# Attention over edges in layer 0: where the edge's direction is multiplied in, and which groups of rows and columns TensorE uses

## The chip, the cores and the metric

The kernel runs on one core of one Trainium2 chip. The metric is device time in microseconds (us), the median of several executions. The profile is one more execution, recorded by the hardware profiler.

## The reference, cut to what matters

A graph network of four layers runs over 6,250 nodes (64 scalars and 32 vectors of three components each, 160 numbers) and 100,000 edges sorted by their end node. Each layer gathers node features at the edges' ends, forms a product with the edge's direction, sums over the edges of each node, and is followed by a layer norm. Only layer 0, attention with four heads, is changed. For each edge with `y0` (a number) and `y1` (three numbers), and weights `w1 = rbf @ W_rbf` (224 columns from 16 inputs):

```
msg      = (source features) + (end features)                      # s: 64, v: 32 x 3
m1_s     = [w_ss*s*y0,  w_vv0*(v . y1)/sqrt3]                      # 96 scalars
m1_v     = [(w_sv*s) y1,  w_vs*v*y0,  w_vv1*(v x y1)/sqrt2]        # 128 vectors
a        = sum over 16 of leaky(m1_s @ W_alpha) * alpha_dot         # 4 heads
alpha    = softmax of a over the edges of one end node
val_s    = m1_s @ Ws_val;   val_v = (m1_v @ Wv_val) * sigmoid(val_s @ Wg);   val_s = sigmoid(val_s)
m2_s, m2_v = the same product of val with y0, y1, and learned constants
h        = [m2_s @ Ws_vlin,  m2_v @ Wv_vlin]                        # per head 16 + 8 x 3
out      = sum over edges of alpha * h, then Wps and Wpv, added to the node
```

## The kernel before, in words

Edges are padded to 784 chunks of 128. The edge loop of layer 0 (`edge_loop0`) takes windows of three chunks (WC = 3, 384 edges), 262 of them, and a window writes to at most 32 consecutive end nodes (WM = 32). It is a software pipeline: step s loads window s, and other parts of the work are done for windows s-2 to s-10 in the same step. Inside `tc.manual_schedule()` the order in which the calls stand in the loop body is the order of each engine's queue; each engine works its queue strictly in that order and waits on semaphores for the others.

The parts of a window, with their lines in the profile:

- `radial` (L1399 to L1417), once in four steps: SP loads the 16 edge inputs and the transposed `y` rows, and POOL multiplies them (L1416), so that a row of 128 partitions holds the inputs times each of the four directions.
- `load` (L1203): POOL gathers three chunks of source features and 32 end-node rows (L722); SP loads the end nodes' numbers, from which `masks` (L1217, DVE) builds `on`, 1 where an edge belongs to a node; `others` (L1222, ACT) makes a large negative number elsewhere.
- `ends` (L1229, PE): end features by a matmul of `on` with the 32 rows. `weights` (L1239, PE): the radial weights for all four directions, in four row groups of 32. `features` (L1249, DVE) adds the ends to the source features.
- `product1` (L1258 to L1263, L1186, L1191): the first product on DVE and POOL, into `tp`, 480 columns.
- `turn` (L1288, L1290): four transposes of a chunk, and ACT's copy `xt`. `linear` (L1296, L1298): the matmuls into `z`, ACT's tanh `th` (L1299) and copy `la` (L1300). `gated` (L1303, DVE). `score` and `spread` (L1314 to L1323).
- `scores`, `exps` (L1330 to L1343): scores by node and edge, their maximum, the exponentials `pT`. `by_edge` (L1352, L1354): `pT` transposed to edges.
- `product2` (L1272 to L1276): the second product, on DVE and POOL, into `m2`, 481 columns (the last is one, for the denominators).
- `sums` (L1359, L1362): `p` times `m2`, over the window's edges. `channels` (L1367 to L1371) turns the sums, `outputs` (L1377 to L1392) multiplies by the last weights, `write` (L735, SP) stores the row.

[...]

The lines that set the gathered rows and PSUM buffers are few:

```
self.wy = self.ps.tile([P, 4, 512], F32, name="wy", bufs=1)
pt = self.ps.tile([P, 4, P], F32, name="t", bufs=2)
z = self.z = self.ps.tile([P, 256], F32, name="z", bufs=1)
self.pa = self.ps.tile([P, 481], F32, name="m", bufs=1)
```

Of the kernel before, what the change touches and what calls it, by code (L numbers as in the profile page):

```python
# [11 lines left out]
I32 = mybir.dt.int32  # L12
# [32 lines left out]
def kernel(ctx: ExitStack, tc: tile.TileContext, t: dict, out: bass.AP):  # L45
# [80 lines left out]
    y_rows = dram.tile([NCH * 4, P], F32, name="y_rows")  # L126
# [11 lines left out]
    with tc.tile_pool(name="prep", bufs=1) as prep:  # L138
# [35 lines left out]
        y4 = prep.tile([P, NCH, 4], F32, name="y4")  # L174
        vec.tensor_copy(y4, y5[:, :, 0:4])
        with tc.tile_pool(name="prep_ps", bufs=2, space=PSUM) as ps, tc.tile_pool(name="prep_sb", bufs=3) as sb:
            for c in range(0, NCH, 32):
                m = min(32, NCH - c)
                pt = ps.tile([P, P], F32, name="pt")
                pe.transpose(pt[0 : 4 * m, :], y4[:, c : c + m, :].rearrange("p c i -> p (c i)"), ident)  # L180
                yt = sb.tile([P, P], F32, name="yt")
                act.copy(yt[0 : 4 * m, :], pt[0 : 4 * m, :])
                nc.sync.dma_start(y_rows[4 * c : 4 * (c + m), :], yt[0 : 4 * m, :])
# [7 lines left out]
    win0G = const.tile([WM, NW0], I32, name="win0G")  # L191
# [3 lines left out]
    with tc.tile_pool(name="win", bufs=1) as sb, tc.tile_pool(name="winp", bufs=1, space=PSUM) as ps:  # L195
# [73 lines left out]
        vec.tensor_copy(win0G, nb[0:WM, :])  # L269
# [912 lines left out]


    def dotted(o, x, n):
        b = x.rearrange("p c i (j k) -> p c (i j) k", k=V)
        vec.tensor_reduce(o[:, 0:n, 3, S:96], b[:, 0:n, 0:9:4, :].rearrange("p c b k -> p c k b"), AX.X, ALU.add)  # L1186

    def crossed(o, x, n, eng):
        b = x.rearrange("p c i (j k) -> p c (i j) k", k=V)
        for k, (p, q) in enumerate(((7, 5), (2, 6), (3, 1))):  # L1190
            eng.tensor_tensor(o[:, 0:n, k, 96:P], b[:, 0:n, p, :], b[:, 0:n, q, :], ALU.subtract)  # L1191

    class Window0:
# [3 lines left out]
        def __init__(self, w, sb, ps, n, yr, at, gi, y, rows, ids, node_idx, dst, tps):  # L1197
            self.w, self.sb, self.ps, self.n = w, sb, ps, n
            self.yr, self.at = yr, at
            self.gi, self.y, self.ids, self.node_idx, self.dst = gi, y, ids, node_idx, dst  # L1200
            self.rows, self.tps = rows, tps

        def load(self):  # L1203
# [3 lines left out]
            self.fw = sb.tile([WM, F], F32, name="fw", bufs=5)  # L1207
# [17 lines left out]
        def ends(self):  # L1225

            self.fd = self.ps.tile([P, WC * F], F32, name="m", bufs=1)
            for c in range(self.n):
                pe.matmul(self.fd[:, c * F : (c + 1) * F], self.on[0:WM, c * P : (c + 1) * P], self.fw, start=True, stop=True)  # L1229

        def weights(self):

            n, w = self.n, self.w
            self.wy = self.ps.tile([P, 4, 512], F32, name="wy", bufs=1)
            half, c0 = self.at
            for c in range(n):
                for i in range(4):
                    q = slice(i * 32, (i + 1) * 32)
                    pe.matmul(  # L1239
                        self.wy[:, i, c * F : (c + 1) * F],  # L1240
                        self.yr[q, (c0 + c) * P : (c0 + c + 1) * P],
                        w["rbf"][q, half, :],
                        start=True,
                        stop=True,
                    )

        def features(self):
            n = self.n
            vec.tensor_add(self.f[:, 0:n, :], self.f[:, 0:n, :], self.fd[:, 0 : n * F].rearrange("p (c q) -> p c q", q=F))  # L1249
            self.tp = next(self.tps[0])  # L1250

        def product1(self):

            n, f = self.n, self.f[:, 0 : self.n]
            o = self.tp.rearrange("p c (b q) -> p c b q", b=4)
            wy = self.wy[:, :, 0 : WC * F].rearrange("p b (c q) -> p c b q", q=F)[:, 0:n]
            x = self.sb.tile([P, WC, 3, 3 * V], F32, name="x1", bufs=2)
            yield vec.tensor_mul(o[:, 0:n, :, 0:S], bc(f[:, :, 0:S], 2, 4), wy[:, :, :, 0:S])  # L1258
            yield vec.tensor_mul(x[:, 0:n], bc(f[:, :, S:F], 2, 3), wy[:, :, 0:3, S:F])
            yield crossed(o, x, n, pool)  # L1260
            fv = f[:, :, S:F].rearrange("p c (j k) -> p c j k", k=V)
            wv = wy[:, :, 3, S:F].rearrange("p c (j k) -> p c j k", k=V)
            yield vec.tensor_mul(o[:, 0:n, 0:3, S:96], fv, wv)  # L1263
            yield dotted(o, x, n)

        def product2(self):

            n, v, y = self.n, self.val[:, 0 : self.n], self.y
            m2 = self.m2 = next(self.tps[1])
            o = m2.rearrange("p c (b q) -> p c b q", b=4)  # L1270
            x = self.sb.tile([P, WC, 3, 3 * V], F32, name="x2", bufs=2)
            yield vec.tensor_mul(o[:, 0:n, :, 0:S], bc(v[:, :, 0:S], 2, 4), bc(y, 3, S))  # L1272
            yield vec.tensor_mul(x[:, 0:n], bc(v[:, :, S:F], 2, 3), bc(y[:, :, 0:3], 3, 3 * V))
            yield crossed(o, x, n, pool)
            vv = v[:, :, S:F].rearrange("p c (j k) -> p c j k", k=V)
            yield vec.tensor_mul(o[:, 0:n, 0:3, S:96], vv, bc(y[:, :, 3:4].to_broadcast([P, n, 3]), 3, V))  # L1276
            yield dotted(o, x, n)

        def turn(self, c):

            if c == 0:
                self.la = self.sb.tile([P, WC, S], F32, name="la", bufs=2)
                self.val = self.sb.tile([P, WC, F], F32, name="val", bufs=3)
                self.th = self.sb.tile([P, WC, 96], F32, name="th", bufs=2)
                self.xt = {}
            pt = self.ps.tile([P, 4, P], F32, name="t", bufs=2)
            for k in range(4):
                pe.transpose(pt[:, k, :], self.tp[:, c, k * P : (k + 1) * P], ident)  # L1288
            self.xt[c] = self.sb.tile([P, 4, P], F32, name="xt", bufs=3)
            act.copy(self.xt[c], pt)  # L1290

        def linear(self, c):

            w, xt = self.w, self.xt.pop(c)
            z = self.z = self.ps.tile([P, 256], F32, name="z", bufs=1)
            pe.matmul(z[:, 0:F], xt[0:96, 3, :], w["ms"], start=True, stop=True)  # L1296
            for k in range(3):
                pe.matmul(z[:, F + k * V : F + (k + 1) * V], xt[:, k, :], w["mv"], start=True, stop=True)  # L1298
            act.activation(self.th[:, c, :], z[:, S:F], AF.Tanh, scale=0.5)  # L1299
            act.copy(self.la[:, c, :], z[:, 0:S])  # L1300

        def gated(self, c):
            vec.scalar_tensor_tensor(  # L1303
                self.val[:, c, S:F].rearrange("p (k v) -> p k v", k=3),
                bc(self.th[:, c, S:96], 1, 3),
                1.0,
                self.z[:, F:256].rearrange("p (k v) -> p k v", k=3),
                ALU.add,
                ALU.mult,
            )  # L1310

        def score(self):
            n, w, sb = self.n, self.w, self.sb
            act.activation(self.val[:, 0:n, 0:S], self.th[:, 0:n, 0:S], AF.Copy, bias=1.0)  # L1314
            vec.scalar_tensor_tensor(self.la[:, 0:n], self.la[:, 0:n], 0.2, self.la[:, 0:n], ALU.mult, ALU.max)
            vec.tensor_mul(self.la[:, 0:n], self.la[:, 0:n], bc(w["adot"], 1, n))
            self.sc = sb.tile([P, WC, 4], F32, name="sc", bufs=2)
            vec.tensor_reduce(self.sc[:, 0:n], self.la[:, 0:n].rearrange("p c (h a) -> p c h a", h=4), AX.X, ALU.add)  # L1318

        def spread(self):  # L1320
            n = self.n
            self.sca = self.sb.tile([P, WC, P], F32, name="sc_all", bufs=2)
            pool.tensor_copy(self.sca[:, 0:n].rearrange("p c (h m) -> p c h m", h=4), bc(self.sc[:, 0:n], 3, WM))  # L1323

        def scores(self):

            n = self.n
            pt = self.ps.tile([P, 4 * P], F32, name="t", bufs=2)
            for c in range(n):
                pe.transpose(pt[:, c * P : (c + 1) * P], self.sca[:, c, :], ident)  # L1330
            self.spt = pt

        def exps(self, old=None):
            n, sb, e, pt = self.n, self.sb, self.n * P, self.spt
            s = sb.tile([P, WC * P], F32, name="s", bufs=2)
            mx = self.row[:, 41:42]
# [10 lines left out]

        def by_edge(self):
            n, e = self.n, self.n * P
# [3 lines left out]
            self.p = self.sb.tile([P, WC * P], F32, name="p", bufs=2)  # L1353
            act.copy(self.p[:, 0:e], pt[:, 0:e])  # L1354

        def sums(self, c):
            if c == 0:
                self.pa = self.ps.tile([P, 481], F32, name="m", bufs=1)
            pe.matmul(self.pa, self.p[:, c * P : (c + 1) * P], self.m2[:, c, 0:481], start=c == 0, stop=c == self.n - 1)  # L1359
            if c == self.n - 1:  # L1360
# [547 lines left out]
```

## Time and profile before

| | |
|---|---|
| time, median of 3 runs | 8017.31 us (8013.19 to 8020.87) |
| the profiled execution | 8008.86 us, its span 8007.1 us |
| mean granted clock of TensorE | 0.948 |
| layer 0's edge loop, first to last transpose (L1288) | 315.0 to 3261.0 us |
| steps between these | 261 |
| DMA, mean over the span | 100 GB/s |

The page names engines: PE is TensorE's matmuls, PEld its weight loads, DVE VectorE, ACT ScalarE, POOL GpSimd, SP SyncE. A line of a group gives line, engine, operation, out<-in, shapes and count, then busy us and the mean ns of one, then the engine's idle time just before and what ended most of it. In a listing by time the first number is the start, the second the length of one or several instructions that follow each other. Matmuls overlap, so the distance from start to start says more of them than the length.

### The profile page before, as it was taken

The numbers are of one execution on the slowest core, as the hardware profiler recorded it, in microseconds if no ns is written. First come the engines' busy times: TensorE is split into PE (matmuls) and PEld (weight loads), VectorE is DVE, ScalarE is ACT, GpSimd is POOL, SyncE is SP. The second block draws the span as 40 slices with busy tenths as digits, with TensorE's granted clock in tenths as the row PEclk, the third lists the DMA queues.
The fourth block names the chain that finished last, engine by engine and source line by source line (L and its number), as shares of the span: only waits on it lengthen the run. The fifth ranks groups of instructions, "written<-read, shape, count | busy, mean of one in ns | idle before, by whom it ended". The sixth has DMA issues, their size and how long they took to land. (4 is left out here: it accounts for less than half of the span.)

```text
span 8007.1 us, 150406 instructions
## 1 busy us (share of the span) xinstructions
PE 7328.2 (92%) x49240; PEld 5720.5 (71%) x49240; DVE 5391.7 (67%) x11871; ACT 3997.6 (50%) x12138; POOL 5269.2 (66%) x5412
## 2 busy tenths in 40 slices
PE   4899999999999999789999999997888887888887
PEld 2677877787878878569999999995555556555556
DVE  5488888878888788557777777775444446555557
ACT  1255555555555555345555555555555554333334
POOL 0377777777777777117777777772777770677771
PEclk9999999999999999669999999996899998999999
DMA  4344444433333333235565656555333335444446
GB/s 137 99 121 111 112 116 119 109 61 63 60 64 60 64 60 63 53 103 99 100 103 98 100 101 100 98 88 144 87 86 86 86 85 178 112 110 110 110 110 228
DMA packets 645090, 799.53 MB, mean 100 GB/s; under 512 B 185122, under 2 KB 512146, under 8 KB 636722
## 3 DMA queue, kind: packets, MB, share of 16 engines
q1 hardware_dynamic: 404818, 501.89, 22.3%
q0 software_dynamic: 238880, 283.36, 20.5%
q8 instruction: 402, 6.59, 0.4%
q14 instruction: 414, 3.39, 0.1%
q10 hardware_dynamic: 576, 4.30, 0.1%
HBM read 548.48 MB, written 240.64 MB: 99 GB/s over the span
## 5 line engine op out<-in xcount | busy, mean ns | idle before, releaser
L722 POOL DMA_INDIRECT f<-feat,r_src x2352 | 2536.4, 1078 | 969.7 <-issue 550.8
L1081 POOL DMA_INDIRECT tab<-o,scat x784 | 1350.4, 1722 | 433.5 <-ACT o L1080 301.5
L857 PE MATMUL pa<-pr,oy 128*128 128x321 f32 (+1 forms) x3136 | 1110.6, 492 | 0.0
L866 ACT COPY o<-pa 32x96 f32<-32x96 f32 (+4 forms) x2358 | 553.3, 245 | 843.4 <-PE pa L857 797.1
L1067 PE MATMUL pt<-same,tp 128*128 128x128 f32 x6272 | 895.5, 286 | 7.0 <-DVE tp L710 4.0
L857 PEld LDWEIGHTS pa<-pr,oy 128*128 128x128 f32 x3136 | 609.4, 199 | 371.0 <-issue 193.7
L1067 PEld LDWEIGHTS pt<-same,tp 128*128 128x128 f32 x6272 | 764.3, 192 | 24.2 <-PE pf L1051 16.3
L1290 ACT COPY xt<-t 128x512 f32<-128x512 f32 x784 | 460.8, 588 | 592.6 <-PE t L1288 568.7
L1359 PE MATMUL m<-m,p 128*128 128x481 f32 x1568 | 739.0, 581 | 0.9 <-ACT row L1390 0.9
L1069 ACT COPY xt<-pt 128x512 f32<-128x512 f32 x784 | 459.6, 586 | 524.3 <-PE pt L1067 524.3
L1298 PEld LDWEIGHTS z<-w_mv,xt 128*128 128x128 f32 x4704 | 622.1, 195 | 0.0
L1078 PE MATMUL po<-ov,xt 128*128 128x32 f32 x4704 | 611.6, 267 | 0.0
L1323 POOL COPY sc_all<-sc 128x384 f32<-128x384 f32 x262 | 302.8, 1156 | 464.2 <-DVE sc L1318 461.3
L1298 PE MATMUL z<-w_mv,xt 128*128 128x32 f32 x4704 | 601.5, 265 | 0.0
L1078 PEld LDWEIGHTS po<-ov,xt 128*128 128x128 f32 x4704 | 588.3, 192 | 0.0
L807 PE MATMUL ww<-w,hid 64*128 64x192 f32 (+1 forms) x2088 | 260.8, 364 | 297.1 <-DVE pr L839 170.7
L1288 PE MATMUL t<-ident,tp 128*128 128x128 f32 x3136 | 513.9, 288 | 0.0
L1288 PEld LDWEIGHTS t<-ident,tp 128*128 128x128 f32 x3136 | 385.3, 152 | 178.1 <-issue 126.1
L807 PEld LDWEIGHTS ww<-w,hid 64*128 64x128 f32 x2088 | 180.8, 189 | 443.9 <-ACT o L866 208.5
L1303 DVE SCALAR_TENSOR_TENSOR val<-th,z 128x96 f32<-128x96 f32 x784 | 196.3, 250 | 406.6 <-ACT la L1300 406.2
L846 DVE TENSOR_TENSOR pr<-f,ww 128x384 f32<-128x384 f32 x131 | 72.7, 555 | 561.8 <-DMA f<-feat,r_src 255.2
L1299 ACT ACTIVATE th<-z 128x96 f32<-128x96 f32 x784 | 197.0, 251 | 433.9 <-PE z L1298 396.3
(328 smaller groups left out, 16509.6 us busy)
## 6 DMA issues: line engine op xcount, KB each, us to landing
tab<-zeros SPq DMA_DIRECT2D x49, 1280.0 KB
nodes<-in_src_row_dram SPq DMA_DIRECT2D x98, 512.0 KB
dn<-in_dst_row_dram SPq DMA_DIRECT2D x261, 192.0 KB
f<-feat,r_src POOLq DMA_INDIRECT x2352
tb<-tab SPq DMA_DIRECT2D x24, 1280.0 KB
e<-in_ef64T_dram SPq DMA_DIRECT2D x196, 128.0 KB
dn<-in_dst_row_dram SPq DMA_DIRECT2D x196, 128.0 KB
e<-in_ef64T_dram SPq DMA_DIRECT2D x261, 96.0 KB
```

Of the source, the lines that this page charges most:

```text
L722: pool.indirect_dma_start(out=o, out_offset=None, in_=table, in_offset=bass.IndirectOffsetOnAxis(ap=idx, axis=0),)
L807: pe.matmul(self.ww[:, q, 0:wn], self.hid[k, c * P : (c + 1) * P], m, start=True, stop=True)
L857: pe.matmul(pa[:, 0:m], self.oy[:, q, :], self.pr[:, q, 0:m], start=c == 0, stop=c == self.ns[h] - 1)
L866: act.copy(o[q, at : at + e], pa[q, b0 * V : b0 * V + e])
L1067: pe.matmul(pt[:, k, :], self.tp[:, c, lo : lo + P], self.same[:, c, :], start=True, stop=True)
L1069: act.copy(self.xt, pt)
L1078: pe.matmul(po[:, 96 + i * V : 96 + (i + 1) * V], xt[:, 1 + i, :], w["ov"], start=True, stop=True)
L1081: pool.indirect_dma_start(out=self.tables[c % len(self.tables)], out_offset=bass.IndirectOffsetOnAxis(ap=self.scat[:, c : c + 1], axis=0), ...
L1288: pe.transpose(pt[:, k, :], self.tp[:, c, k * P : (k + 1) * P], ident)
L1290: act.copy(self.xt[c], pt)
L1298: pe.matmul(z[:, F + k * V : F + (k + 1) * V], xt[:, k, :], w["mv"], start=True, stop=True)
L1359: pe.matmul(self.pa, self.p[:, c * P : (c + 1) * P], self.m2[:, c, 0:481], start=c == 0, stop=c == self.n - 1)
```

## The change

All of it lies in layer 0.

- The weights are no longer multiplied by the directions beforehand. `radial` multiplies the inputs by `y0` alone, and lays the three chunks of a window in three row groups of 32 (16 rows times `y0`, 16 without). The gather of end rows brings them three times (96 rows), and `ends` makes end features and weights in three row groups, into three banks `wf`.
- The first product multiplies features by weights only (384 columns in `tp` instead of 480), but for the dot product, which DVE and POOL make with `y1`. `linear` multiplies three transposed pieces by a wider weight (480 columns), and DVE multiplies the columns that need a direction by it (`q`) and adds; `joined` adds what is left, `gates` and `gated` apply the gate.
- The scores come from two matmuls with 384 columns (`leaky`: W_alpha and its negative, then Relu; `scores`: alpha_dot spread over the nodes), in place of DVE's operations, POOL's spread and transposes.
- The second product is gone. `by_edge` multiplies the transposed exponentials by `y0` (ACT) and `y1` (DVE), 512 columns a chunk. `sums(0)` multiplies the first 128 value channels with them, summed over three chunks; `sums(1)` the last 32, each chunk in its own column group. `outputs` has 32 matmuls of 40 columns, one column group for each head, with weights that hold all constants; `denominators` sums `pT` on DVE.
- The pipeline has one stage less, and the order of the calls in a step is new. The weights' preparation stands ahead of the node phase. The other loop over late edges follows the same parts.

```
         def ends(self):
-            self.fd = self.ps.tile([P, WC * F], F32, name="m", bufs=1)
...
+            self.wf = self.ps.tile([P, WC, 512], F32, name="wf", bufs=1)
             for c in range(self.n):
...
+                q = slice(c * WM, (c + 1) * WM)
+                pe.matmul(self.wf[:, c, 0:F], self.on[q, c * P : (c + 1) * P], self.fw[q, :], start=True, stop=True)
+            for c in range(self.n):
+                q = slice(c * WM, (c + 1) * WM)
+                pe.matmul(self.wf[:, c, F : F + 224], self.yr[q, :], self.w["rbf"][q, :], start=True, stop=True)
...
         def product1(self):
...
+            yield vec.tensor_mul(d, fv, bc(self.y[:, :, 1:4], 3, V))
+            pool.tensor_add(d[:, :, 0, :], d[:, :, 0, :], d[:, :, 1, :])
+            pool.tensor_add(d[:, :, 0, :], d[:, :, 0, :], d[:, :, 2, :])
+            yield vec.tensor_mul(o[:, :, 0:2, 0:S], bc(f[:, :, 0:S], 2, 2), w[:, :, 0:128].rearrange("p c (b k) -> p c b k", k=S))
+            yield vec.tensor_mul(o[:, :, :, 96:P], fv, bc(w[:, :, 128:160], 2, 3))
+            yield vec.tensor_mul(o[:, :, 2, 0:96].rearrange("p c (j k) -> p c j k", k=V), fv, bc(w[:, :, 192:224], 2, 3))
+            yield vec.tensor_mul(o[:, :, 0, S:96], d[:, :, 0, :], w[:, :, 160:192])
...
         def turn(self, c):
...
+            for k in range(3):
+                pe.transpose(pt[:, k * P : (k + 1) * P], self.tp[:, c, k * P : (k + 1) * P], ident)
+            act.copy(self.xt[:, :, c, :], pt[:, 0 : 3 * P].rearrange("p (k e) -> p k e", k=3))
...
         def linear(self, c):
...
+            z = self.ps.tile([P, 512], F32, name="z", bufs=1)
+            for k, (lo, hi) in enumerate(((0, 128), (128, 256), (256, 480))):
+                pe.matmul(z[:, lo:hi], self.xt[:, k, c, :], w[:, lo:hi], start=True, stop=True)
+            act.activation(self.th[:, c, :], z[:, 0:96], AF.Tanh, scale=0.5)
...
+            vec.tensor_mul(
+                q.rearrange("p b (k v) -> p b k v", k=3), z4[:, 1:4, 0:96].rearrange("p b (k v) -> p b k v", k=3), turns
+            )
+            x = q[:, 0, :].rearrange("p (k v) -> p k v", k=3)
+            vec.tensor_add(x, x, z4[:, 0:3, 96:P])
+
+        def joined(self):
...
+            vec.tensor_add(q[:, :, 1, :], q[:, :, 1, :], q[:, :, 2, :])
+            pool.tensor_add(q[:, :, 0, :], q[:, :, 0, :], q[:, :, 1, :])
+
+        def gates(self):
...
+            act.activation(self.gt[:, 0:n], self.th[:, 0:n, S:96], AF.Copy, bias=1.0)
+            act.activation(self.val[:, 0:n, 0:S], self.th[:, 0:n, 0:S], AF.Copy, bias=1.0)
+
+        def gated(self):
...
+            vec.tensor_mul(v, q, bc(self.gt[:, 0:n], 2, 3))
+
+        def leaky(self):
...
+            pe.matmul(pt[:, 0:e], self.w["alpha"], self.xt[:, 0, 0:n, :].rearrange("p c e -> p (c e)"), start=True, stop=True)
...
+            act.activation(self.lt[:, 0:e], pt[:, 0:e], AF.Relu)
...
         def scores(self):
...
+            pe.matmul(self.spt[:, 0:e], self.w["adot"], self.lt[:, 0:e], start=True, stop=True)
...
+        def denominators(self):
+            vec.tensor_reduce(self.row[:, 40:41], self.pT[:, 0 : self.n * P], AX.X, ALU.add)
...
         def by_edge(self):
...
+            for c in range(n):
+                act.activation(self.py[:, c, 0, :], pt[:, c * P : (c + 1) * P], AF.Copy, scale=self.y[:, c, 0:1])
+            p = pt[:, 0 : n * P].rearrange("p (c m) -> p c m", m=P)
+            vec.tensor_mul(self.py[:, 0:n, 1:4, :], bc(p, 2, 3), bc(self.y[:, :, 1:4], 3, P))
...
+        def sums(self, k):
...
+            pa = self.ps.tile([P, 512], F32, name="m", bufs=2)
+            for c in range(n):
+                py = self.py[:, c].rearrange("p i m -> p (i m)")
+                if k == 0:
+                    pe.matmul(pa, self.val[:, c, 0:P], py, start=c == 0, stop=c == n - 1)
+                else:
+                    pe.matmul(pa[c * V : (c + 1) * V, :], self.val[:, c, P:F], py, start=True, stop=True)
...
+            act.copy(self.a[k][0:r].rearrange("p i m -> p (i m)"), pa[0:r])
...
         def outputs(self, old=None):
...
+            for i in range(4):
+                for k, rows in enumerate((P, r)):
+                    for h in range(4):
+                        q = slice(h * WM, (h + 1) * WM)
+                        pe.matmul(
+                            po[q, :],
+                            self.a[k][0:rows, i, q],
+                            w["o"][k][0:rows, i, h, :],
+                            start=i == 0 and k == 0,
+                            stop=i == 3 and k == 1,
+                        )
+            act.copy(row[:, 0:40], po)
...
+    def radial(sb, yb, c0, n, it):
...
+        for c in range(min(WC, n)):
+            m = -(-(n - c) // WC)
+            for h in range(2):
+                nc.sync.dma_start(yr[32 * c + 16 * h : 32 * c + 16 * h + 16, 0:m, :], e[:, c:n:WC, :])
+            nc.sync.dma_start(yb[32 * c : 32 * c + 16, 0:m, :], y[:, c:n:WC, :].to_broadcast([16, m, P]))
...
+                pool.tensor_tensor(yr[q, g, :], yr[q, g, :], yb[q, g, :], ALU.mult)
```

The order of a step, after:

```
+                    at(9).write(tabs[0][(s - 9) % tab_n[0]])
                     on(load)
                     x3.ends()
+                    x3.features()
+                    x7.sums(0)
+                    x5.gates()
+                    on(first)
                     chunk(x4, 0, "turn")
+                    x5.joined()
+                    x5.scores()
+                    on(first)
+                    x5.exps()
+                    on(first)
+                    chunk(x4, 0, "linear")
+                    on(load)
+                    chunk(x4, 1, "turn")
+                    on(first, 2)
+                    x7.sums(1)
+                    chunk(x4, 1, "linear")
                     x3.others()
                     chunk(x4, 2, "turn")
                     x6.by_edge()
+                    x5.denominators()
+                    chunk(x4, 2, "linear")
+                    x8.outputs()
+                    x5.gated()
                     x2.masks()
+                    x4.leaky()
                     on(load, 3)
```

## The prediction

> **What bounds the kernel now.** I read the page first, then the busy times by stretch, then TensorE's order of time in one step, then who waits. The changed code is the edge loop of layer 0; the other layers' loops stay.
>
> ```profile
> span 8007.1 us, 150406 instructions
> PE 7328.2 (92%) x49240; PEld 5720.5 (71%) x49240; DVE 5391.7 (67%) x11871; ACT 3997.6 (50%) x12138; POOL 5269.2 (66%) x5412
> PEclk9999999999999999669999999996899998999999
> ```
>
> The loop's own stretch (columns: start:end, length, busy us and count of PE, weight loads, DVE, ACT, POOL, then granted clock, DMA share, GB/s):
>
> ```profile
> 600.00:3000.00 2400.00, 2378.94 (x19133) 1919.00 (x19132) 1930.95 (x4468) 1300.73 (x4037) 1844.02 (x2397) 0.97 0.37 83
> ```
>
> PE is busy 99% of it, DVE 80%, POOL 77%, ACT 54%: the loop ends when PE ends. One step in order of time (start, length, engine, line):
>
> ```profile
> 1700.76 0.97 PE L1359 MATMUL m<-m,p 128*128 128x481 f32 x2
> 1701.57 0.60 PE L1288 MATMUL t<-ident,tp 128*128 128x128 f32 x4
> 1702.00 1.78 PE L1359 MATMUL m<-m,p 128*128 128x481 f32 x4
> 1703.62 0.44 PE L1296 MATMUL z<-w_ms,xt 96*128 96x160 f32 x2
> 1703.89 0.75 PE L1298 MATMUL z<-w_mv,xt 128*128 128x32 f32 x6
> 1704.48 0.64 PE L1288 MATMUL t<-ident,tp 128*128 128x128 f32 x4
> 1704.95 0.49 PE L1352 MATMUL t<-ident,pT 128*128 128x128 f32 x3
> 1705.28 0.33 PE L1377 MATMUL m<-w_ls,aT 96*128 96x64 f32 x2
> 1705.45 0.81 PE L1379 MATMUL m<-w_lv,aT 128*128 128x32 f32 x6
> ...
> 1707.60 1.08 PE L1229 MATMUL m<-fw,on 32*128 32x160 f32 x6
> 1708.61 0.66 PE L1288 MATMUL t<-ident,tp 128*128 128x128 f32 x4
> 1709.19 1.10 PE L1239 MATMUL wy<-w_rbf,yr 32*128 32x160 f32 x24
> 1710.22 0.54 PE L1296 MATMUL z<-w_ms,xt 96*128 96x160 f32 x2
> ...
> 1711.55 0.97 PE L1359 MATMUL m<-m,p 128*128 128x481 f32 x2
> ```
>
> From start to start a step is 1711.55 - 1700.76 = 10.79 us without a gap. The first and last transposes of the loop stand at 315.0 and 3261.1 us, 261 steps apart: 11.29 us a step on average. What lies between is a longer step in every fourth (VectorE's product at L1273 goes from 1.05 to 2.58 us beside POOL's 1.80 us product of `radial`) and stretches at a lower clock (0.97 on average, so at most 3% of 2,946, 88 us).
>
> Prices, start to start, are read here: an fp32 matmul is two instructions and takes 0.81 us for 481 columns (1.69 ns a column); one of 32 columns takes 0.59/3 = 0.20; a transpose 0.11; six 32-row instructions in one row group 1.01; 24 of them in four row groups 1.03.
>
> ```profile
> L1290 ACT COPY xt<-t 128x512 f32<-128x512 f32 x638 | 375.0, 588 | 468.2 <-PE t L1288 448.6
> L1303 DVE SCALAR_TENSOR_TENSOR val<-th,z 128x96 f32<-128x96 f32 x637 | 159.5, 250 | 320.3 <-ACT la L1300 319.9 <-PE t L1288 0.3
> L1362 ACT COPY a<-m 128x481 f32<-128x481 f32 x212 | 118.2, 557 | 11.7 <-PE m L1359 11.7
> L1263 DVE TENSOR_TENSOR tp<-f,wy 128x288 f32<-128x288 f32 x213 | 94.7, 445 | 0.0
> ```
>
> L1303 needs `th` and `z`, yet waits for the copy `la`, which only shares `z`'s PSUM bank. Today such waits cost nothing, because PE has other work queued.
>
> **What the Trainium skill says.** "TensorE: Matmul & The Clock Gate", Measured speedup vs the span model: 3 column groups of 32 at 512 columns run 2.38 times as fast as one after the other, 4 row groups 3.07 times. The trace agrees for rows (24 instructions in 1.03 us, against 4 x 1.01 at L1229's rate: 3.9 times); no line of it has column groups. "TensorEngine Tiling (Array Packing)", Key Properties: a change of tiling mode drains TensorE. The trace fits: 1.03 us is six slots of 0.135 (160 of 1.69/2 ns) and some 0.21 more. "PSUM — Partial Sum Buffer", PSUM bank collisions raise a hardware error: accesses of two engines to one bank are kept apart, reads too. L1303's 319.9 us of waiting for `la` agrees.
>
> **The change, part by part, per step of three chunks.**
>
> PE. Removed: all of the 10.79. Put in its place:
> - end features and weights, three row groups: two slots of 0.135, two of 0.19 (224 columns), 0.21 of switch: 0.87 (was 1.01 + 1.03);
> - `sums(0)`, 3 x 512 columns: 3 x 0.86 = 2.58 (was 2.43);
> - nine transposes instead of twelve, 1.05 (was 1.5);
> - `linear`, 3 x 480 columns: 3 x 0.81 = 2.43 (was about 2.7);
> - `leaky` and `scores`, 384 columns each: 1.29 (was 0.36);
> - `by_edge` 0.33, as before; the 0.56 of channel transposes goes;
> - `sums(1)`, 3 matmuls of 512 columns in three column groups: two slots of 0.43 and 0.21 to switch, 1.07 (2.58 / 2.38 = 1.08 by the skill). Bounds: 0.9, and 2.6 if the groups go one after the other;
> - `outputs`, 32 matmuls of 40 columns, 64 instructions in four column groups (was 0.81). Bounds: 16 slots of 0.034 and the switch, 0.75; 64 at the 0.043 of L1239, 2.75. The skill's LDWEIGHTS section has weight loads go with the columns, a quarter here of L1298's 0.1, in sequence 1.7. I take 1.4.
> Sum 11.0 against 10.79. PE's own work does not fall.
>
> DVE. Gone are the second product (0.95, 1.05 to 2.58, 0.54, 0.47), the large first one and the score (3 x 0.35). New, at about 1 ns an element and 0.07 us: 0.37 + 0.47 + 0.37 + 0.37 + 0.17 for product 1, 3 x 0.54 behind the linear part, 0.37 `joined`, 0.47 denominators, 1.27 for the 1,152 weighted elements in `by_edge`, 0.37 `gated`. With features, mask and exps 7.4 us, from 8.7. ACT: some 6.4, from 6.2. POOL: six differences (2.6 us), the spread (1.16) and 1.80/4 go; two sums of 96 (0.8), one of 288 (about 0.9) and 1.2/4 come: 6.4, from 8.3. All of these are below PE, so they cost nothing by themselves; what counts is their order.
>
> The hand-offs. Each queue runs in its written order. I laid one step out by hand from `ends` at 0:
> - PE does ends to 0.87, `sums(0)` to 3.45, turn 0 to 3.8, `scores` to 4.45. ACT must first copy `sums(0)` (from 3.65, 0.48 to the next start), then two gate activations (0.18, 0.28), and only then turn 0's copy, to 5.1. PE's `linear(0)` waits from 4.45 to 5.15. Queued behind it: everything on PE, and DVE's work on z.
> - PE then goes 5.95, turn 1 6.3, `sums(1)` 7.35, `linear(1)` 8.15, turn 2 8.5, `by_edge` 8.85. ACT's tanh of chunk 1 starts at 8.4; mask copy (`others`), turn 2's copy and three scaled copies of `by_edge` follow to 10.05. PE's `linear(2)` waits until 9.5.
> - DVE's 1,152 elements read the bank of those scaled copies, so they start at 10.1 and end at 11.35; denominators 11.8, chunk 2 12.45, `gated` 12.8, `masks` 13.3. The next `ends` needs that mask. PE, done with `outputs` (11.7) and `leaky` (12.35), waits 0.95.
> That is 13.3; with the first weight load after a stall, which nothing covers, 13.4. A stalled PE thus idles 2.4 us of 13.4. What is late next is `ends`, and with it the whole following step.
>
> [...] I let the clock be full; were 0.97 kept, 0.03 x 3,500 = 105 us more. The fourth step's 0.75 goes as well: `radial`'s product meets an idle DVE. Both are inside the 11.29 that I compare with.
>
> SP and the rest. `radial` issues 9 DMAs instead of 16 in four steps (0.42 us each); SP spends over half of the loop waiting for rows, so nothing. `write` and its wait move one step earlier. The gather of end rows brings 96 rows for 32: 0.87 us to at most the 0.97 of 128 rows, on POOL with room. Before the loop: 7 transposes and stores of y instead of 25 (about 0.67 us each, 12 us less), about 71 weight DMAs instead of 43 (13 us more, now ahead of the node phase, on SP under DVE's window work; uncovered they would cost those 13), some 24 scalings on DVE, 4 us. I take -10 to +20 together, +5.
>
> Sum: (13.4 - 11.29) x 261 = 551; 8008.9 (the profiled execution; its span is 8007.1) + 551 + 5 = 8565. The median of the runs is 8 us above that execution, within its own scatter: 8570.
>
> **Rivals.**
> - Shorter chain: DVE need not stand behind ACT in `by_edge`, PE waits only for turn copies. 12.4 us a step: 8009 + 1.1 x 261 = 8300. For it: the layout has no slack there; against: L1303's wait.
> - The change doesn't do what it says: column groups run one after the other. `sums(1)` + 1.5, `outputs` up to 2.75: 14.9 to 15.6, 8950 to 9130. For it: no precedent in the trace; against: the skill's 2.38.
> - PE stays the bound without stalls: the windows' lags cover every hand-off, as they do now, and `outputs` costs its lower bound: 10.4 to 10.6 a step, 7800. It decides once PE idles less than 0.3 us a step beside 11.0 of work (or 0.9 beside 10.4). Against: ACT's order puts a copy that nobody needs before the next step ahead of the one that PE needs at once.
> Waits that just eat the gain end at 8010.
>
> **How the numbers follow.** The main case has 0.50 (8420 to 8720), the shorter chain 0.20, serial columns 0.15, the unstalled PE 0.13, no change 0.02. Faster by over 0.2% (about what these runs, 8013 to 8021, can tell) 0.13; within 0.02; slower 0.85. The range 8200 to 8980 leaves out the faster case and the far end of the serial one.
>
> **What would show it.** Right: PE below 90% in the loop, its weight loads for `linear` waiting for ACT's `xt`, and for `ends` for DVE's `on`; steps near 13.4; clock 1.0. Wrong: PE at 99% (then only its sum counts), or `sums(1)` near 2.6 us, or DVE's wide product in `by_edge` starting before ACT's last scaled copy.

## Result and profile after

The changed kernel takes 8642.28 us in the median (8634.97 to 8647.37, 4 runs) against 8015.33 for the kernel before (8013.19 to 8020.87, 4 runs): a ratio of 1.078, 95% interval 1.0762 to 1.0799. The forecast was 8570, range 8200 to 8980. The profiled execution took 8644.81 us. Its page:

```profile
span 8643.1 us, 162500 instructions
PE 7381.0 (85%) x57622; PEld 5128.6 (59%) x57622; DVE 5154.6 (60%) x11624; ACT 3978.8 (46%) x11599; POOL 4479.4 (52%) x4367
PEclk9999999999999999995899999999599998999999
```

The same stretch of the loop as before (start:end, length, busy us and count of PE, weight loads, DVE, ACT, POOL, then granted clock, DMA share, GB/s):

```profile
600.00:3000.00 2400.00, 1997.29 (x21251) 1185.58 (x21251) 1414.04 (x3486) 1056.94 (x2966) 986.81 (x1264) 1.00 0.25 68
```

PE is busy 83% of it where it was 99%, at a full clock where it was 0.97; every other engine is below 60%. No engine is the bound: PE waits for others, and they wait for PE. The transposes of the loop run from 309.4 to 3897.1 us (before: 315.0 to 3261.0), 261 steps apart, so a step takes 13.75 us for 11.29. The whole difference is there: the loop starts 5.6 us earlier, is 641.7 us longer, and from its last transposes to the end of the span it is 4746.0 us, for 4746.1 before.

One step on TensorE in order of time (start, length, engine, line, operation; in brackets how long it was idle before, and what ended that):

```profile
1700.52 1.09 PE L1268 MATMUL z<-w_m,xt 128*128 128x128 f32 x6 [0.50 <-ACT xt L1260]
...
1701.87 1.06 PE L1351 MATMUL m<-py,val 128*32 128x512 f32 x6
...
1705.16 1.06 PE L1268 MATMUL z<-w_m,xt 128*128 128x128 f32 x6 [0.56 <-DVE q L1278]
1706.15 0.81 PE L1365 MATMUL m<-w_o,a 128*32 128x40 f32 x64
1706.89 0.91 PE L1301 MATMUL t<-xt,w_alpha 128*128 128x384 f32 x2
1709.06 0.55 PE L1226 MATMUL wf<-fw,on 32*128 32x160 f32 x6 [1.25 <-DVE on L1212]
...
1709.91 2.84 PE L1349 MATMUL m<-py,val 128*128 128x512 f32 x6
...
1714.23 1.09 PE L1268 MATMUL z<-w_m,xt 128*128 128x128 f32 x6 [0.50 <-ACT xt L1260]
```

From `linear(0)` to `linear(0)`: 13.71 us, with three gaps where there was none: 0.50, 0.56 and 1.25, together 2.31. They stand at the three places where the prediction put its waits. (The lines left out are transposes, the other `linear`, the radial half of `ends` and `scores`.) The largest is before `ends`, which needs the mask `on`. What keeps VectorE from making that mask earlier is seen in its own order of time:

```profile
1705.83 1.36 DVE L1340 TENSOR_TENSOR py<-t,r_y 128x1152 f32<-128x1152 f32 x1 [0.82 <-ACT py L1338]
...
1708.22 0.45 DVE L1296 TENSOR_TENSOR val<-q,gt 128x288 f32<-128x288 f32 x1
1708.59 0.41 DVE L1212 TENSOR_SCALAR on<-dn,win0F 128x384 f32<-128x384 int32 x1
```

and in ScalarE's, just before it:

```profile
1704.90 0.90 ACT L1338 ACTIVATE py<-t,r_y 128x128 f32<-128x128 f32 x3
```

DVE's wide product reads the PSUM bank (a buffer of `t` with the transposed exponentials) that ACT's three scaled copies read. They end at 1705.80, it starts at 1705.83. Behind it stand the denominators, two operations on `q`, `gated`, and then, last in the queue, the comparison that makes the mask, which depends on none of them. The groups of instructions between 600 and 3000 us show it as a rule (busy us, mean ns of one, then idle before and its releaser; 174 or so steps):

```profile
L1274 DVE TENSOR_TENSOR q<-z,yc 128x288 f32<-128x288 f32 x524 | 238.0, 454 | 319.3 <-ACT th L1269 319.3
L1340 DVE TENSOR_TENSOR py<-t,r_y 128x1152 f32<-128x1152 f32 x174 | 236.2, 1358 | 142.2 <-ACT py L1338 142.2
```

`q` (L1274) reads other columns of `z` than the tanh does, and needs nothing that the tanh makes. It waits for it all the same, as L1303 waited for `la` before: in the step shown, the matmuls of `linear(0)` end at 1701.61, the tanh runs from 1701.64 to 1701.89, and `q` starts at 1701.93. So about 0.32 us of each wait is the tanh's; the rest of the 319.3 us is waiting for the matmuls, although the profile puts all of it to the tanh, which ends last. Here this wait is on the way to the next matmul on `z`.

### The profile page after: what moved, and what is told of

The parts are those of the page before. It is cut to its first block, busy times and chain, and to the rows that moved or that the text cites. A ratio compares the mean times of both kernels' runs of the same rounds, so it can differ in the third digit from the quotient of the medians.

```text
span 8643.1 us, 162500 instructions
## 1 busy us (share of the span) xinstructions
PE 7381.0 (85%) x57622; PEld 5128.6 (59%) x57622; DVE 5154.6 (60%) x11624; ACT 3978.8 (46%) x11599; POOL 4479.4 (52%) x4367
## 5 line engine op out<-in xcount | busy, mean ns | idle before, releaser
L722 POOL DMA_INDIRECT f<-feat,r_src x2352 | 2311.4, 983 | 1030.7 <-issue 610.6
L1284 POOL TENSOR_TENSOR q<-q 128x288 f32<-128x288 f32 x262 | 207.6, 792 | 1842.4 <-DVE q L1283 1842.4
L1268 PE MATMUL z<-w_m,xt 128*128 128x128 f32 (+1 forms) x4704 | 853.3, 318 | 280.4 <-DVE q L1278 143.2
L1268 PEld LDWEIGHTS z<-w_m,xt 128*128 128x128 f32 x4704 | 586.7, 191 | 713.0 <-ACT xt L1260 713.0
L1356 ACT COPY a<-m 128x512 f32<-128x512 f32 (+1 forms) x524 | 305.6, 583 | 1314.8 <-PE m L1349 1176.1
L1349 PE MATMUL m<-py,val 128*128 128x512 f32 x1568 | 751.3, 616 | 3.5 <-DVE py L1340 3.5
L1274 DVE TENSOR_TENSOR q<-z,yc 128x288 f32<-128x288 f32 x784 | 356.2, 454 | 481.6 <-ACT th L1269 481.6
L1340 DVE TENSOR_TENSOR py<-t,r_y 128x1152 f32<-128x1152 f32 x262 | 354.9, 1355 | 219.6 <-ACT py L1338 219.6
L1349 PEld LDWEIGHTS m<-py,val 128*128 128x128 f32 x1568 | 279.3, 191 | 331.2 <-issue 327.1
L1226 PE MATMUL wf<-fw,on 32*128 32x160 f32 x1568 | 144.5, 348 | 353.1 <-DVE on L1212 330.1
L1316 DVE CUSTOM_DVE_ANT_0 s<-t,off 128x384 f32<-128x384 f32 x262 | 145.8, 556 | 465.3 <-PE t L1309 465.3
```

The source lines that it names most:

```text
L722: pool.indirect_dma_start(out=o, out_offset=None, in_=table, in_offset=bass.IndirectOffsetOnAxis(ap=idx, axis=0),)
L1268: pe.matmul(z[:, lo:hi], self.xt[:, k, c, :], w[:, lo:hi], start=True, stop=True)
L1274: vec.tensor_mul(q.rearrange("p b (k v) -> p b k v", k=3), z4[:, 1:4, 0:96].rearrange("p b (k v) -> p b k v", k=3), turns)
L1340: vec.tensor_mul(self.py[:, 0:n, 1:4, :], bc(p, 2, 3), bc(self.y[:, :, 1:4], 3, P))
L1349: pe.matmul(pa, self.val[:, c, 0:P], py, start=c == 0, stop=c == n - 1)
```

## The experiments

Theory: a chain over ACT and DVE, in the order in which the calls are written, sets the step; TensorE's own work is about 11 us. Rivals: the new matmuls themselves are too slow, or one wait alone is to blame.

For each kernel the step is the time between the first and the last start of the weight loads of `ends` (L1226; before L1229), divided by 261. The first seven edited kernels ran where the kernel before is slower too (8855.46 and a median of 8863.81 us). Their clock was 0.88 to 0.90 between 4000 and 7800 us, in the layers after the loop, where it was 0.93 for the changed kernel; between 600 and 3000 us it was 0.99 or 1.00. So of them the loop's steps are compared, not the totals that the expectations also give.

| kernel | first and last start, us | step, us | PE busy in 600 to 3000 |
|---|---|---|---|
| before | 306.3, 3251.0 | 11.28 | 99% |
| after | 300.8, 3882.3 | 13.72 | 83% |
| masks early | 301.3, 3544.3 | 12.43 | 91% |
| outputs twice | 300.9, 3974.0 | 14.07 | 85% |
| vector first | 300.6, 3940.4 | 13.95 | 83% |
| gates first | 300.4, 3820.3 | 13.49 | 85% |
| new order | 301.0, 3522.8 | 12.34 | 91% |
| new order, outputs twice | 302.6, 3677.4 | 12.93 | 92% |
| new order, one column group | 301.7, 3985.7 | 14.11 | 96% |
| no stalls | 301.5, 3146.6 | 10.90 | 100% |
| turns together | 299.9, 3231.1 | 11.23 | 98% |

**Masks early.** The mask is made before the third turn instead of at the end of the step; nothing else is moved.

```
+                    x2.masks()
                     chunk(x4, 2, "turn")
...
-                    x2.masks()
```

> The changed kernel with one call moved: masks of the window after next goes ahead of turn 2 instead of behind gated. Chain of hand-offs: TensorE's wait of 1.5 us for the mask ahead of `ends` goes, a step falls from 13.72 to 12.0 to 12.3 us, 8190 to 8280 us in all. Rival, the new matmuls themselves are too long: the step stays within 0.1 us, 8615 to 8670.

Measured: 12.43, 1.29 us less for one call moved. In order of time, PE's scores are now followed by `ends` with no gap:

```profile
1711.68 0.91 PE L1301 MATMUL t<-xt,w_alpha 128*128 128x384 f32 x2
1712.52 0.55 PE L1226 MATMUL wf<-fw,on 32*128 32x160 f32 x6
```

The wait for the mask cost what its gap shows, 1.25, and the two waits for `linear` stay. Over 261 steps it is 337 us, a little less than the 363 to 453 expected, because I had taken the wait for 1.5. So more than half of the 2.44 us by which a step had grown came from the place of one 0.4 us operation in DVE's queue.

**Outputs twice.** The output products are issued twice over; the second pass starts its sums anew, so the result is the same.

```
-            for i in range(4):
+            for i in (0, 1, 2, 3, 0, 1, 2, 3):
```

> The changed kernel with the 64 instructions of `outputs` issued twice, the second pass starting its sums anew, so the result is the same: 0.74 us more of TensorE work in each step. Chain of hand-offs: it fills part of the 1.5 us in which TensorE waits for the mask, 8610 to 8680. Rival, TensorE's own work sets the step: 261 x 0.74 = 193 us more, 8835.

Measured: 14.07, 0.35 more, between the two. The 64 further instructions took 0.60 (1712.82 to 1714.16 is 1.34, for 0.74). One step:

```profile
1712.82 1.40 PE L1365 MATMUL m<-w_o,a 128*32 128x40 f32 x128
1714.16 0.91 PE L1301 MATMUL t<-xt,w_alpha 128*128 128x384 f32 x2
1715.73 0.55 PE L1226 MATMUL wf<-fw,on 32*128 32x160 f32 x6 [0.66 <-DVE on L1212]
```

Here the gap before `ends` shrank from 1.25 to 0.66 by what the products added, and the step stayed at 13.77 (1701.96 to 1715.73): the mask's time is set elsewhere, as the theory has it. But in most steps something is added. In the next one, of 14.12 us, ACT's scaled copies start 0.31 us after the copy of `xt` ahead of them instead of overlapping its end, and the mask is late by that. The profile names the transposes of L1335 as what they waited for, which are long done; what held them isn't shown. Between 600 and 3000 us 125 of 169 steps have this pause, with a median of 14.11, and the 44 without it have 13.77; the changed kernel has it in none. TensorE still waits for the mask, 0.79 us a step on average, so its own work doesn't set the step with the pause either. The chain's forecast holds where the pause is absent.

**Vector first.** In `by_edge` DVE's wide product is issued ahead of ACT's three scaled copies, so the order at the bank is turned round.

```
+            p = pt[:, 0 : n * P].rearrange("p (c m) -> p c m", m=P)
+            vec.tensor_mul(self.py[:, 0:n, 1:4, :], bc(p, 2, 3), bc(self.y[:, :, 1:4], 3, P))
             for c in range(n):
                 act.activation(self.py[:, c, 0, :], ...)
-            p = ...
-            vec.tensor_mul(...)
```

> The changed kernel with two statements of by_edge swapped: VectorE's product of 1,152 stands ahead of ScalarE's three scaled copies, both read the same PSUM bank. Chain with one engine at a time in a bank: VectorE no longer waits 0.8 us for ScalarE, but ScalarE's copies now wait 1.3 us and hold back the tanh of chunk 2; 8560 to 8640. Rival, they may read the bank together: about 1.0 us less in a step, 8380.

Measured: 13.95, 0.23 more; neither. The wait went to the other side. ACT's timeline, then two lines of DVE's, in one step:

```profile
1713.82 0.88 ACT L1340 ACTIVATE py<-t,r_y 128x128 f32<-128x128 f32 x3 [1.72 <-DVE py L1338]
```

```profile
1712.43 1.36 DVE L1338 TENSOR_TENSOR py<-t,r_y 128x1152 f32<-128x1152 f32 x1 [0.33 <-PE t L1335]
...
1714.88 0.46 DVE L1274 TENSOR_TENSOR q<-z,yc 128x288 f32<-128x288 f32 x1 [0.63 <-ACT th L1269]
```

ACT is now idle for 1.72 us until DVE's product ends at 1713.79, the tanh of the third chunk is queued behind its copies, and DVE waits for that tanh 0.63 before it gets to the mask. Both orders use the bank for 2.3 us in a row; what stands last in either queue pays. So the rival, 1.0 us less, is excluded. That the step is longer, and not a little shorter as the chain has it, goes with a pause like the one above: in 122 of 170 steps, as here, DVE's product starts 0.2 to 0.4 us after DVE is free and the transposes are done (median 13.92), and in the 48 steps without it the median is 13.59, 0.13 less than in the changed kernel and within what the chain expected.

**Gates first.** The two gate activations go from between the first sums and turn 0 to before the first sums, so that ACT comes to turn 0's copy earlier.

```
+                    x5.gates()
                     x7.sums(0)
-                    x5.gates()
```

> The changed kernel with one call moved: gates ahead of sums(0), so 0.43 us of ScalarE's work no longer stands between the copy of sums(0) and the copy that TensorE's linear(0) waits for. Chain: the tanh of chunk 0 then waits behind the exponentials, and the mask stays last; 20 us less, 8590 to 8650. Rival, every wait of TensorE adds to the step: 0.43 x 261 = 112 us less, 8530.

Measured: 13.49, 0.23 less, in the middle of the two on average. In order of time `linear(0)`, the last line, no longer waits, and the mask's gap is unchanged:

```profile
1706.92 0.55 PE L1226 MATMUL wf<-fw,on 32*128 32x160 f32 x6 [1.25 <-DVE on L1212]
...
1711.73 1.09 PE L1268 MATMUL z<-w_m,xt 128*128 128x128 f32 x6
```

The average hides two kinds of steps. Of 177 between 600 and 3000 us, 135 take 13.35, 0.37 less; 34 take 13.73, because in most of these the tanh of the second chunk starts some 0.3 us late, with no cause that the profile shows, and `linear(2)` waits longer by that. So in the common step most of the 0.50 gap is gained, which is nearer to the rival (0.43) than to my expectation (0.08): a wait of TensorE that is taken out comes off the step nearly whole, as the mask's did.

**New order.** Only the order of the calls is changed: masks ahead of `by_edge`, the first sums behind the three turns, the output products last in the step.

```
 t0 ends gates load features first scores first others z0 t1 t2 exps s0 joined
 load first(3) gated load z1 masks by_edge denominators load leaky s1 z2 load outputs
```

> Only the order of the calls in the hand-laid step differs from the changed kernel: the same instructions, the masks right after the transposes, the output products at the end of the step, the scaled copies before the turn they used to follow, the other edges' vector work between the gates. The reading of the profile so far (a chain across ACT and DVE sets 13.72 us a step, PE has only about 10.6 us of issue in it): TensorE becomes the bound, over 95% busy between 600 and 3000 us against 83%, the step falls to 10.4 to 10.8 us, the whole to 8643 + (10.6 - 13.72) x 261, about 7830 us (7780 to 7900), faster than both kernels and about 0.975 of the kernel before. The rival (the new products themselves are slower than what they replace, the order hardly matters) expects a step above 12.9 us and over 8430 us.

Measured: 12.34, PE busy 91%. On its chip it took 8960.15 us, a ratio of 1.0109 (1.0071 to 1.0148) to the kernel before. Better than the changed kernel by its steps, and a miss of the expectation by 1.7 us. The timeline has two new gaps:

```profile
1713.81 0.57 PE L1365 MATMUL m<-w_o,a 128*32 128x40 f32 x39
1714.83 0.49 PE L1365 MATMUL m<-w_o,a 128*32 128x40 f32 x25 [0.44 <-issue]
1715.24 0.55 PE L1259 MATMUL t<-ident,tp 128*128 128x128 f32 x3
...
1719.21 0.55 PE L1259 MATMUL t<-ident,tp 128*128 128x128 f32 x3 [0.57 <-ACT xt L1260]
```

The third turn waits 0.57 us for ACT's copy of the second: `t` has two PSUM buffers, and the scores hold the other one until the softmax has read them (tested in the last experiment). And the output products pause in their middle, so that they take 1.43 us (1713.81 to 1715.24) for 0.74. I first put that pause to ACT's copy of the second sums; but that copy ends at 1713.49, before the products begin. What it is the profile doesn't show.

**New order, outputs twice.** As the new order, with the output products issued twice. The expectation calls the output another; as in the first such kernel, the second pass starts its sums anew, and the result is the same.

> The reordered step with the output products issued twice over (the same values summed twice, so the output is another). If TensorE is the bound in the new order, the whole of what the products add (0.60 us in the kernel with the old order) is now in the step, where the old order took in 0.35 of it: 0.60 x 261 = 157 us above the reordered kernel. If some other engine's chain still sets the step: under 0.3 us a step, under 80 us.

Measured: 12.93, 0.59 more than the new order, the whole of what the products add, where the old order had taken in some of it. TensorE bounds this order, pauses included.

**New order, one column group.** The second sums accumulate in one column group, and the output products read 32 rows of them instead of 96.

```
-                    pe.matmul(pa[c * V : (c + 1) * V, :], self.val[:, c, P:F], py, start=True, stop=True)
+                    pe.matmul(pa[0:V, :], self.val[:, c, P:F], py, start=c == 0, stop=c == n - 1)
```

> The reordered step with the second sums of all chunks accumulated in one column group instead of one group for each chunk; the result is the same. If the column groups work side by side (0.99 us for six instructions of 512 columns, against 2.68 us for the six of the first sums), the six come one after another: 2.68 - 0.99 = 1.7 us more a step, about 440 us above the reordered kernel. If the groups do not matter: no difference.

Measured: 14.11, 1.77 more.

```profile
1708.88 2.76 PE L1351 MATMUL m<-py,val 128*32 128x512 f32 x6
1711.57 1.09 PE L1268 MATMUL z<-w_m,xt 128*128 128x128 f32 x6
1712.59 1.72 PE L1365 MATMUL m<-w_o,a 128*32 128x40 f32 x64
```

The six instructions take 2.69 (1708.88 to 1711.57) instead of 0.99: 1.70, as expected. So the three column groups do work side by side. The output products changed as well: 1.66 for 1.43, now that tiles of 32 rows alternate with tiles of 128, and with no pause that the timeline shows.

**No stalls.** From the new order three more calls are moved: the softmax's vector part ahead of the first `linear` (so that its PSUM buffer is free), the first sums between the second and the third turn, the second sums ahead of `leaky`.

```
 t0 ends gates load features first scores first others exps z0 t1 joined s0
 load first(3) gated t2 load z1 masks by_edge s1 denominators load leaky z2 load outputs
```

> The reordered step, with the vector part of the softmax ahead of the first linear, the first sums between the second and the third turn, and the second sums ahead of the leaky product: the two waits of the first reordered kernel (0.44 us of the outputs for ACT's copy of the second sums, 0.57 us of the third turn for ACT's copy of the second) should go. If those two are all that TensorE still waits for, the step is 12.27 - 0.44 - 0.57, about 11.25 us in the median, TensorE is above 97% busy between 600 and 3000 us, and the kernel is level with the kernel before on its chip (0.995 to 1.01), because TensorE's own work per step is then about 11.2 us in both: the change took next to nothing off it. If TensorE had the 10.6 us of work first thought of, the step falls to 10.6 and the ratio to 0.98. If a new wait takes their place: a step of 11.8 or more, ratio above 1.01.

Measured: 7893.26 us (7889.85 to 7897.4, 5 runs) against 8017.03 for the kernel before in the same session (9 runs): a ratio of 0.9844, interval 0.9831 to 0.9858. It is faster than both kernels. Its engines on the page, and then its stretch:

```profile
PE 7246.1 (92%) x57622; PEld 5174.8 (66%) x57622; DVE 5163.2 (65%) x11624; ACT 3979.3 (50%) x11599; POOL 4561.7 (58%) x4367
```

```profile
600.00:3000.00 2400.00, 2400.00 (x26731) 1531.71 (x26730) 1788.22 (x4387) 1324.91 (x3728) 1309.63 (x1590) 1.00 0.32 78
```

PE has the same 57,622 instructions as the changed kernel and no gap in the stretch; the step is 10.90. I had expected 11.25, because I had taken only the visible 0.44 off the output products: all 0.69 was lost time (12.27 in the median, less 0.57 and 0.69, is 11.01), and a part of it, about 0.2, is still there in most steps (0.96 for `outputs`, 1711.40 to 1712.36, in one step; 0.74, 1700.61 to 1701.35, in the one before).

**Turns together.** As the kernel without stalls, but the third turn right behind the second.

> As the kernel without the two waits, but the third turn straight after the second again, with the vector part of the softmax still ahead of both. If the third turn waited because the scores held the other PSUM buffer until the softmax's vector part had read them: no wait now either, the step within 0.1 us of the other kernel. If it waits for something else of the second turn, 0.4 to 0.6 us more a step.

Measured: 11.23, 0.33 more, less than the second case and more than the first (in the median 11.26 for 11.00).

```profile
1711.85 0.55 PE L1259 MATMUL t<-ident,tp 128*128 128x128 f32 x3 [0.21 <-DVE row L1316]
```

The third turn now waits for the softmax's vector part (L1316), not for the copy of the second turn: the buffer that the scores held is the one it takes, and DVE empties it 0.21 us late. That confirms the explanation: the softmax's vector part stands earlier than in the new order, and not yet early enough.

## Why the prediction was right

**The chain and its three waits: right.** They are where they were put, and idle 2.31 us of a step, for 2.4 forecast. Masks early and gates first each took one away, and no stalls took all three with the same instructions. Sizes: the wait of `linear(0)` 0.50 (0.70 forecast), of `linear(2)` 0.56 (0.65), of `ends` 1.25 (0.95). The last is longer mainly because ACT's scaled copies take 0.90 for three; the layout left them less than 0.6 (9.5 to 10.05). At `linear(2)` the profile names DVE's addition to `q`, I had named ACT's copy of `xt`; they end at 1705.01 and 1705.02, so the trace doesn't tell them apart, and no run did.

**DVE behind ACT at the bank: right.** The rival of a shorter chain (12.4 us, 8300) rested on its absence. Vector first shows that the two take turns in either order. This step rested on the Trainium skill's "PSUM — Partial Sum Buffer" (PSUM bank collisions raise a hardware error), by which two engines' reads of one bank have to be kept apart as well. The trace agrees that they are: 142.2 us of waiting at L1340, and reads that start 0.03 us after the other engine's end, in both orders. The error itself no run shows.

**TensorE's own sum: right as a whole, 11.0 for a measured 10.90** in the one kernel where nothing else counts. That it fits so well is luck, because it is made of misses that cancel. `outputs` takes 0.74 to 0.96, at the lower bound, not 1.4: 64 instructions of 40 columns in four column groups go at 11.6 ns each (0.74 / 64), so the reckoning by weight loads one after another was wrong. Against that, in the kernel without stalls, `leaky` and `scores` take 0.75 each for 0.65, the three `linear` 2.58 for 2.43, and the transposes 1.56 with `by_edge`'s for 1.38: three of them take 0.33 in a row and 0.47 ahead of `ends`, where the tiling changes. `ends` (0.85 for 0.87), `sums(0)` (2.57 for 2.58) and `sums(1)` (0.99 for 1.07) were right. For `sums(1)` the factor of the Trainium skill ("TensorE: Matmul & The Clock Gate", Measured speedup vs the span model: 2.38 for three column groups) was on the safe side: 2.69 / 0.99 = 2.7 here, as it was for four row groups in the kernel before (3.07 there for 512 columns, 3.9 for 160 by the lines in the prediction, where I wrote that the two agree). This excludes the rival of serial columns; its price (1.5 for `sums(1)`) was nearly right, 1.70. The upper end of that rival's step, 15.6, isn't worked out in the prediction; 14.9 is 13.4 and 1.5.

**The rival of an unstalled TensorE** was right on what it needs, gaps below 0.3 us a step, and the changed kernel doesn't have it. An order that does gave 7893, not 7800, as a step of 10.90 and not 10.5 must.

**The clock and the fourth step: right.** The clock was 1.00 in the loop, for 0.97; why, no run shows. Every fourth step is longer by only 0.07 us (13.78 for 13.72), where it was 0.75. By its instructions alone no order wins: 10.90 is no less than the 10.79 of a gapless step before. The kernel without stalls is ahead by 0.38 us a step of the mean of 11.28, which held the slower stretches and the fourth steps. No run took the two apart.

**Before the loop: wrong by 11 us.** +5 forecast, 5.6 us earlier measured. If the 12 us of fewer transposes were gained in full, most of the 13 us of further weight DMAs and of the 4 of scalings can't have been on the path; which of them wasn't looked at.

**The 72 us between 8570 and 8642** (80 between the sum, 8565, and the profiled execution) are the step: 13.75 for 13.4, 0.35 x 261 = 91, less the 11 us before the loop. The gaps don't hold them (2.31 for 2.4), but TensorE's work between the gaps, 11.40 in the step shown, by start to start: `linear` 2.84 for 2.43 (0.92 to 0.99 each, also the one that follows no wait; what makes it slower isn't shown); `leaky` and `scores` 1.73 for 1.29, because a wait follows each, so that its whole length counts (0.75 from start to start in the kernel without stalls); transposes and `by_edge` 1.57 for 1.38; `sums(0)` 2.68 for 2.58; against these `outputs` 0.74 for 1.4 and `sums(1)` 0.99 for 1.07. So the gain at `outputs` was more than used up by prices that were too low elsewhere.

## What to carry to other kernels

When the work is re-cut between engines, lay out one step of the queues by hand before counting busy time: an operation that the next step's first matmul needs must not stand last in a queue behind the slowest hand-off. Two engines that read one PSUM bank were a hand-off in either order here (2.3 us in a row), and a PSUM buffer stays taken until its reader has been issued and done (waits of 0.57 and 0.21 us), so place the reader before the next user. If no engine is busy all the time at a full clock, reorder before you judge a change: the same instructions here gave 8642 us with TensorE 83% busy in the loop and 7893 us with no gap in it.

## What the runs showed of the hardware that I had not expected

- Small matmuls in four column groups are cheap: 64 instructions with 40 columns in 0.74 us, and 64 more for 0.60. In the kernel with one column group for the second sums, where tiles of 32 rows and of 128 alternate, the same number took 1.66; that the alternation is the cause wasn't tried apart.
- A pause without a wait: in the new order the output products stop in their middle in 192 of 193 steps (0.44 us put to "issue" in the step shown, about 0.83 in every fourth), and the pause is there again when they are issued twice. It is absent in the changed kernel, where TensorE has just waited 0.56 us, and also in the kernel without stalls, where it has not; with the outputs twice in the old order, 26 of 170 steps have one, mostly of 1.0 us and more. Whether the supply of instructions is behind it wasn't tried.
- A pause of about 0.3 us on ACT or DVE at an operation whose inputs the profile shows as done: at the readers of the transposed exponentials in outputs twice (125 of 169 steps) and vector first (122 of 170), at a tanh in gates first (30 of 177), in no step of the changed kernel. Its cause is open, and it is as large as the differences between these kernels.
- Three scaled copies of 128 columns take 382 ns each on ACT, 0.90 together, when the wide copy of 384 columns takes 472.
